# A graph layer whose edges go two ways: 113 picked windows of edges for 100, and 865 gathered chunks for 1125

## The chip, the cores and the metric

The kernel runs on one core of a Trainium2 chip. Its engines each work through their own queue in order: TensorE (PE in the profile; its weight loads are shown apart as PEld), VectorE (DVE), ScalarE (ACT), GpSimd (POOL), and SyncE (SP), which only issues transfers. The metric is the device time of one execution in microseconds (us); several executions of each kernel are timed.

## What is computed

A graph layer over 12,500 nodes of 128 features and 400,000 edges. The edges are sorted by their destination (`dst`), the sources (`src`) are random.

```
Xs  = X[src]
msg = where(edge_type == 0, Xs @ W_data.T + b_data, Xs @ W_control.T + b_control)
agg = segment_sum(msg, dst)
out = relu(agg + X @ W_self.T + b_self)
x   = layernorm(x + out)
```

The kernel sums the source rows first, by destination and by type, and multiplies the sums by the weights afterwards; the number of edges of each type per node, which the biases need, is counted beside it.

## The kernel before

**Data.** The edges are cut into 3125 chunks of 128 (`NC`), in 25 groups of 125 chunks (`NG`, `GC`). A group covers about 500 nodes (`GN`). Each row of x is held as three bf16 parts (384 values, 768 bytes), in SBUF as `x3` and in device memory as `rows3`. The sums of a group stand in a tile `acc` (two types of feature sums, two of counts), 640 nodes wide with a lap into the next group.

**Two ways to sum a chunk.** Each group is cut into windows in turn: a gathered window (kind "p") of 12 or 11 chunks and a picked window (kind "e") of 20 chunks, four of each (`PC`, `EC`, `NE`).

- *Gathered* (`gathered`): for each chunk GpSimd fetches the 128 source rows from `rows3` by an indirect transfer into a tile `msg` (L700); DVE makes for the whole window the 0/1 matrix `psel` that says which edge goes to which of 24 nodes and which type; PE adds the rows with three matmuls of 48 columns (L658) and counts with one (L712) into a bank `sums`. There are 24 `msg` tiles (`AHEAD`), so GpSimd can run ahead.
- *Picked* (`picked`, with `give_slots`): the 2560 edges of a window are sorted by the block of 128 nodes that their source lies in, into 100 cells of 32 places. DVE makes the matrices for that (O, prod, half, rm, rv), PE makes ranks and cells (`rk`), ScalarE copies them, and a broadcast transfer of 800 KB hands the result to all partitions as `pick`. Then PE picks the source rows out of `x3` itself, with 98 matmuls of 384 columns into `got` (L732), four cells at a time; ScalarE copies two results at a time into `emsg` (L743), 12 copies a window; PE adds these by the matrix `esel` with 75 matmuls of 176 columns (L658) and counts with 25 (L761). Edges that find no place in their cell go to 64 spare rows, fetched by one more gather (L747). If a window has more than 64 of these, or a lane more than 7, the flag `bad` is set and a slow path over all 3125 chunks (`long_path`) makes the result.

Both kinds end with a DVE addition of the bank `sums` into `acc` (`accumulate`, L688). The pool of `sums` has two banks, for both kinds together.

**Order.** The program walks over the picked windows w (`pairs`, 100 of them). `merged` weaves into each: its own seven turns of picks, copies and sums, the rank work for the windows w + 2 and w + 3, and the gathered chunks whose place falls there. The chunks are spread evenly over the windows from w = 2 on (`LAG`). Once both kinds of a group are done, the remainder list `rest` holds its lap (`pass_on`) and its finish: load x, turn it, multiply by the three weights and the biases (tile `fin`, L850), normalise, write. The last group is finished in two parts, as its windows close (`soon`).

SP issues the loads of edge data (`load`), the first destination of each window (`first_i`, `near_i`), the transfers `there` and `pick`, the reads of x and the writes of the result.

Of the kernel before, what the change touches and what calls it, by code (L numbers as in the profile page):

```python
# [22 lines left out]
GC = 125  # L23
NG = NC // GC
GN = P * GC * N // E
PC = (12, 11, 11, 11)
PB = 12
EC = 20
CQ = EC // 4
NE = len(PC)  # L30
NWIN = 2 * NE
LAG = 2
DPC = P * N // E
PAD = 10
PW = DPC + 2 * PAD
EW = 88
AW = PW + DPC * (PB - 1)
WMAX = max(AW, EW)
M0 = 50
R = 640  # L40
# [3 lines left out]
NCELL = 4 * NQ  # L44
OVF = 64
TOP = 7
AHEAD = 24
ACC_ROWS = 99 * P
EPS = 1e-5

assert sum(PC) + NE * EC == GC and NC % GC == 0 and NBLK == NCELL - 2 and max(PC) == PB
# [97 lines left out]
def short_path(ctx, tc, const, ident, eps, wT, brow, bad, x, src, dst, etype, ws, bs, out):  # L149
# [12 lines left out]
    def windows(g):  # L162

        c = g * GC
        for i, n in enumerate(PC):
            yield "p", i, c, n
            yield "e", i, c + n, EC
            c += n + EC

    def edges(a, c, n):  # L170
        return a[c * P:(c + n) * P].rearrange("(p c) -> p c", c=n)

    rows_p = NE * PB
    raw = {}
    starts = {k: [c for kind, _, c, _ in windows(0) if kind == k] for k in "pe"}
    assert all(b - a == 31 for k in "pe" for a, b in zip(starts[k][k == "p":], starts[k][1 + (k == "p"):]))

    def load(g, kind):
        names = ("src", "dst", "typ")
        if kind == "e":  # L180
            raw[kind, g] = [ld.tile([P, NE, EC], I32, name=f"e{name}") for name in names]
            c = g * GC + starts["e"][0]
            for t, a in zip(raw[kind, g], (src, dst, etype)):
                at = a[c * P:(c + 31 * (NE - 1)) * P].rearrange("(i k) -> i k", k=31 * P)[:, :EC * P]
                nc.sync.dma_start(out=t[:, :NE - 1, :], in_=at.rearrange("i (p c) -> p i c", c=EC))
                nc.sync.dma_start(out=t[:, NE - 1, :], in_=edges(a, c + 31 * (NE - 1), EC))
        else:
            raw[kind, g] = [ld.tile([rows_p, P], I32, name=f"p{name}") for name in names]
            c = g * GC
            for t, a in zip(raw[kind, g], (src, dst, etype)):  # L190
                nc.sync.dma_start(out=t[:PB, :], in_=a[c * P:(c + PB) * P].rearrange("(c p) -> c p", p=P))
                for i in range(1, NE):
                    b = c + starts["p"][i]
                    nc.sync.dma_start(
                        out=t[i * PB:(i + 1) * PB, :], in_=a[b * P:(b + PB) * P].rearrange("(c p) -> c p", p=P)
                    )


# [15 lines left out]
    near_i = keep.tile([rows_p, NG], I32, name="near_i")  # L214
    for kind, i, c, _ in windows(0):
        if kind == "p":
            nc.sync.dma_start(
                out=near_i[i * PB:(i + 1) * PB, :],
                in_=dst.rearrange("(o g e) -> o g e", o=1, g=NG)[:, :, c * P].to_broadcast([PB, NG]),
            )  # L220
    load(0, "p")

# [109 lines left out]

    worst = keep.tile([P, 3, P], FP, name="worst")
    nc.vector.memset(worst, 0.0)
    over_n = keep.tile([P, NG * NE], BF, name="over_n")

    halves = tmp.tile([1, 2, NG * NWIN], I32, name="halves")
    nc.vector.memset(x3[:, NBLK - 1], 0.0)
# [164 lines left out]
        return [over_before, over_matrix, turn, keep]  # L503

    def give_slots(w):
        g, i = divmod(w, NE)
        blk, blk2, node2, code2, pk = (t[:, i * EC:(i + 1) * EC] for t in codes["e", g])
        s = {}

# [135 lines left out]
        return [(0.6 + a / 1000, lambda a=a: half(a, a + h)) for a in range(0, NCELL, h)]  # L645


    acc, added = {}, []

    def sums():  # L650
        return ps2.tile([P, 512], FP, name="sums")
# [23 lines left out]

    def pass_on(g):

        if g + 1 < NG:
            begin_acc(g + 1)
            added.append(nc.vector.tensor_add(acc[g + 1][:, :, :lap], acc[g + 1][:, :, :lap], acc[g][:, :, GN:]))  # L680

    def accumulate(g, i, ps, wide, width):

        begin_acc(g)
        with tc.issue_after(added[-2].ins) if len(added) > 1 else ExitStack():
            at = nc.vector.value_load(place_i[0:1, g, i:i + 1], min_val=0, max_val=R - WMAX)
        win = acc[g][:, :, bass.ds(at, width)]
        added.append(nc.vector.tensor_add(win, win, ps[:, :4 * wide].rearrange("p (a w) -> p a w", w=wide)[:, :, :width]))  # L688

    def gathered(g, i):  # L690
        n = PC[i]
        s = {}

        def choose():
            sel = sp.tile([P, n, 2 * PW], BF, name="psel")
            s["sel"] = select(sel, near_col, codes["p", g][1][:, i * PB:i * PB + n])

        def chunk(c):
            msg = mp.tile([P, 3 * D], BF, name="msg")
            nc.gpsimd.indirect_dma_start(  # L700
                out=msg, out_offset=None, in_=rows3[:, :],
                in_offset=bass.IndirectOffsetOnAxis(ap=codes["p", g][0][:, i * PB + c:i * PB + c + 1], axis=0),
            )
# [8 lines left out]
            nc.tensor.matmul(cnt, one_col, sel, start=False, stop=(c == n - 1), skip_group_check=True)  # L712
            if c == n - 1:
                accumulate(g, 2 * i, s["ps"], AW, PW + DPC * (n - 1))

        return evenly([lambda c=c: chunk(c) for c in range(n)])

    def picked(w, tiled):

        g, i = divmod(w, NE)  # L720
        s = {"sel": {}, "msg": {}}
        per, pair = 4, 2

# [72 lines left out]

    soon = {NE - 2: (0, 1), NE - 1: (2, 3, 4)}
    assert (starts["p"][NE - 1]) * DPC - PAD >= 2 * (P - 3)  # L800

    def finish(g, ks):
        full = P - 3
# [115 lines left out]


    chunks, closed, rest = {}, {}, []
    for p in range(pairs):
        g, i = divmod(p, NE)
        for c, (_, u) in enumerate(gathered(g, i)):
            at = LAG + (p + (c + 0.5) / PC[i]) * (pairs - LAG) / pairs
            chunks.setdefault(int(at), []).append((at % 1, u))
        closed.setdefault(int(at), []).append(p)

    for w in range(pairs):
        g, i = divmod(w, NE)  # L930
# [193 lines left out]
```

## Time and profile before

| what | value |
|---|---|
| time, median of 3 runs | 2387.49 us (2369.49 to 2400.51) |
| profiled execution: its time / its span | 2371.03 us / 2369.3 us |
| granted TensorE clock, mean | 0.909 |
| gathers (L700), count and mean | 1125, 1147 ns |
| spare-row gathers (L747), count and mean | 100, 1181 ns |
| copies got to emsg (L743), count and mean | 1200, 804 ns |
| additions into acc (L688), count and mean | 200, 470 ns |
| psel (L463), 11 chunks: count and mean | 75, 427 ns |

A line of the profile's groups reads: line of the kernel, engine, operation, tile written and tiles read, count, then busy time and mean of one, then the engine's idle time just before them and what ended it. "issue" stands for idle time in which the profile shows nothing that was waited for. Matmuls overlap, so that the durations of single ones add up to more than PE's time.

### The profile page before, as it was taken

How to read it: one execution, taken by the hardware profiler on the slowest of the kernel's cores; microseconds unless marked ns; L12 is line 12 of the kernel's file. 1: busy time of each engine (PE TensorE's matmuls, PEld its weight loads, DVE VectorE, ACT ScalarE, POOL GpSimd, SP SyncE). 2: the span in 40 equal slices, each digit the busy share in tenths (PEclk: the TensorE clock that was granted, in tenths of full speed). 3: DMA queues.
4: the chain of work that ended last, by engine and by line, in shares of the span. 5: the costliest groups of instructions: out<-in, count | busy, mean ns of one | idle time of the engine just before them, and what ended most of it. 6: DMA issues, size and time to landing. Idle time of an engine off the chain costs nothing.

```text
span 2369.3 us, 70786 instructions
## 1 busy us (share of the span) xinstructions
PE 1863.1 (79%) x28867; PEld 1364.9 (58%) x28867; DVE 1584.0 (67%) x4224; ACT 1229.7 (52%) x2322; POOL 1412.5 (60%) x1243
## 2 busy tenths in 40 slices
PE   0468887887878787888888887888888888887977
PEld 0346665665556565666565565665666665665646
DVE  6747676766666666767676766676667666676753
ACT  3435554555445545545555554555555555545635
POOL 0366665756465565665666665566666665676661
PEclk9879898999889899999999988998989999999979
DMA  7423342333333333333323323333323323233321
GB/s 206 148 80 104 97 107 84 109 91 98 87 96 96 100 100 90 109 97 94 108 85 106 107 86 102 97 98 106 107 83 104 102 88 102 89 101 105 97 87 42
DMA packets 185017, 236.73 MB, mean 100 GB/s; under 512 B 80295, under 2 KB 152282, under 8 KB 184682
## 3 DMA queue, kind: packets, MB, share of 16 engines
q0 software_dynamic: 57200, 115.59, 17.7%
q1 hardware_dynamic: 114418, 109.94, 14.8%
q10 hardware_dynamic: 13064, 6.60, 1.0%
q8 instruction: 228, 3.74, 0.7%
q14 instruction: 107, 0.88, 0.1%
HBM read 215.35 MB, written 16.64 MB: 98 GB/s over the span
## 4 chain that ended last, share of the span: by engine, by line
PE 66%; issue 10%; ACT 10%; DVE 6%; another core or an unknown queue 5%; DMA 1%; SPq 1%; DVEq 0%; ACTq 0%; POOL 0%; POOLq 0%
PE sums L658 32%; PE got L732 22%; ACT emsg L743 9%; PE fin L850 3%; PE rk L601 2%; PE sums L761 2%; PE rk L489 1%; PE sums L712 1%; DVE esel L463 1%; PE rk L537 1%; DVE x L249 1%; PE rk L621 1%; DVE xt L247 0%; PE fin L837 0%
## 5 line engine op out<-in xcount | busy, mean ns | idle before, releaser
L700 POOL DMA_INDIRECT msg<-rows,pidx x1125 | 1290.4, 1147 | 790.3 <-PE sums L658 363.4
L743 ACT CAST emsg<-got 128x768 bf16<-128x768 f32 x1200 | 919.8, 804 | 796.5 <-PE got L732 328.8
L732 PE MATMUL got<-x,pick 128*32 128x384 bf16 x9800 | 659.2, 353 | 238.7 <-ACT emsg L743 145.6
L658 PE MATMUL sums<-esel,emsg 128*128 128x176 bf16 x7200 | 751.3, 255 | 48.6 <-issue 46.0
L658 PEld LDWEIGHTS <-emsg 128*128 128x128 bf16 x7200 | 579.8, 104 | 220.0 <-issue 215.4
L463 DVE TENSOR_TENSOR esel<-code_col,code 128x1408 bf16<-128x1408 bf16 (+1 forms) x300 | 275.0, 917 | 348.9 <-PE sums L658 195.7
L732 PEld LDWEIGHTS <-pick 128*32 128x32 bf16 x9800 | 242.3, 97 | 421.3 <-issue 336.0
L658 PE MATMUL sums<-psel,msg 128*128 128x48 bf16 x3375 | 240.0, 187 | 48.0 <-issue 35.3
L658 PEld LDWEIGHTS <-msg 128*128 128x128 bf16 x3375 | 187.8, 99 | 77.6 <-issue 72.5
L747 POOL DMA_INDIRECT last<-rows,idx x100 | 118.1, 1181 | 139.4 <-DMA pdst<-in_dst_dram 91.4
L712 PE MATMUL sums<-psel,one_col 128*128 128x48 bf16 x1125 | 184.5, 185 | 16.9 <-issue 16.8
L688 DVE TENSOR_TENSOR acc<-acc,sums 128x352 f32 (+1 forms) x200 | 94.0, 470 | 132.5 <-PE sums L658 54.0
L761 PE MATMUL sums<-esel,one_col 128*32 128x176 bf16 x2500 | 168.2, 254 | 16.2 <-issue 14.7
L463 DVE TENSOR_TENSOR O<-cell_col,blk 128x2000 bf16<-128x2000 bf16 x100 | 119.3, 1193 | 55.7 <-PE got L732 27.8
L643 DVE TENSOR_SCALAR pick<-pick,lane_f 128x1600 bf16<-128x1600 bf16 x200 | 125.6, 642 | 14.2 <-DMA pick<-there 13.7
L601 PE MATMUL rk<-rv,O 128*128 128x64 bf16 x2000 | 89.0, 198 | 50.3 <-DVE rv L589 35.0
L761 PEld LDWEIGHTS <-one_col 128*32 128x32 bf16 x2500 | 84.2, 103 | 63.7 <-issue 31.1
L547 DVE TENSOR_REDUCE ahead<-rk 128x100 bf16<-128x500 f32 x100 | 67.5, 675 | 78.7 <-PE got L732 55.7
L712 PEld LDWEIGHTS <-one_col 128*128 128x128 bf16 x1125 | 109.6, 97 | 18.0 <-issue 17.7
L551 DVE TENSOR_TENSOR prod<-O,ahead 128x2000 bf16<-128x2000 bf16 x100 | 119.0, 1190 | 0.0
L601 PEld LDWEIGHTS <-O 128*128 128x128 bf16 x2000 | 73.4, 101 | 67.3 <-issue 54.8
L631 ACT CAST code<-rk 128x50 bf16<-128x50 f32 x100 | 20.3, 203 | 173.8 <-PE got L732 68.0
(170 smaller groups left out, 1998.4 us busy)
## 6 DMA issues: line engine op xcount, KB each, us to landing
pick<-there SPq DMA_DIRECT2D x100, 800.0 KB
msg<-rows,pidx POOLq DMA_INDIRECT x1125
rows<-x SPq DMA_DIRECT2D x6, 1344.0 KB
xs<-in_x_dram SPq DMA_DIRECT2D x99, 62.5 KB
out_dram<-h SPq DMA_DIRECT2D x99, 62.5 KB
xt<-in_x_dram ACTq DMA_DIRECT2D x6, 896.0 KB
psrc<-in_src_dram SPq DMA_DIRECT2D x100, 6.0 KB
pdst<-in_dst_dram SPq DMA_DIRECT2D x100, 6.0 KB
```

Source lines behind the costliest of these rows:

```text
L463: nc.vector.tensor_tensor(sel.rearrange("p n (w t) -> p n w t", t=2), col[:rows].rearrange("p (o w t) -> p o w t", o=1, t=2).to_broadcast( ...
L551: nc.vector.tensor_tensor(prod, s["O"], ahead.rearrange("p (o j) -> p o j", o=1).to_broadcast([P, EC, NCELL]), op=OP.mult)
L601: nc.tensor.matmul(s["rk"][:m, :2 * CAP], s["held"][:, c * NCELL:c * NCELL + m], s["rv"][:, c].rearrange("p v r -> p (v r)"), start=(c == ...
L643: nc.vector.tensor_scalar(t, t, lane_f, None, op0=OP.is_equal)
L658: nc.tensor.matmul(out, msg[:, j * D:(j + 1) * D], sel, start=(start and j == 0), stop=stop, skip_group_check=True)
L688: added.append(nc.vector.tensor_add(win, win, ps[:, :4 * wide].rearrange("p (a w) -> p a w", w=wide)[:, :, :width]))
L700: nc.gpsimd.indirect_dma_start(out=msg, out_offset=None, in_=rows3[:, :], in_offset=bass.IndirectOffsetOnAxis(ap=codes["p", g][0][:, i * P ...
L712: nc.tensor.matmul(cnt, one_col, sel, start=False, stop=(c == n - 1), skip_group_check=True)
L732: nc.tensor.matmul(ps[CAP * a:CAP * (a + 1), :], slots[w]["pick"][:, a * NQ + q, :], x3[:, 4 * q + a - a0].rearrange("p j d -> p (j d)"), ...
L743: nc.scalar.copy(msg, ps[:, :, :3 * D])
L747: nc.gpsimd.indirect_dma_start(out=msg[:OVF, :], out_offset=None, in_=rows3[:, :], in_offset=bass.IndirectOffsetOnAxis(ap=slots[w]["idx"], ...
L761: nc.tensor.matmul(cells_of(s["ps"], EW, 1)[CAP * (q % 4):CAP * (q % 4 + 1), :], one_col[:, :CAP], s["sel"][q], start=(q < 4), stop=(q + 4 ...
```

## The change

Every group has five gathered windows and five picked ones now, of 5 and 20 chunks in turn (`PB`, `EC`, `NE`). In groups with an odd number the last picked window is left out, and its 20 chunks join the gathered window ahead of it, which then has 25 chunks (`PL`). So even groups have 5 picked windows and 25 gathered chunks, odd ones 4 and 45: in all 13 x 5 + 12 x 4 = 113 picked windows and 13 x 25 + 12 x 45 = 865 gathered chunks.

```
-PC = (12, 11, 11, 11)
-PB = 12
+PB = 5
+PL = 25
 EC = 20
-NE = len(PC)
+NE = 5
...
-AHEAD = 24
+AHEAD = 17
...
+    def of_p(g, i):
+        return PL if g % 2 and i == NE - 1 else PB
...
+    each_e = [(g, i) for g in range(NG) for i in range(NE - g % 2)]
...
     def gathered(g, i):
-        n = PC[i]
+        n = of_p(g, i)
...
-            sel = sp.tile([P, n, 2 * PW], BF, name="psel")
+            sel = sp.tile([P, PL, 2 * PW], BF, name="psel")[:, :n]
...
     def picked(w, tiled):
-        g, i = divmod(w, NE)
+        g, i = each_e[w]
...
-    soon = {NE - 2: (0, 1), NE - 1: (2, 3, 4)}
+    soon = {NE - 2: (0, 1, 2), NE - 1: (3, 4)}
...
-    pairs = NG * NE
+    pairs = len(each_e)
...
-    for p in range(pairs):
-        g, i = divmod(p, NE)
-        for c, (_, u) in enumerate(gathered(g, i)):
-            at = LAG + (p + (c + 0.5) / PC[i]) * (pairs - LAG) / pairs
+    total = sum(of_p(g, i) for g in range(NG) for i in range(NE))
+    n = 0
+    for p in range(NG * NE):
+        for _, u in gathered(*divmod(p, NE)):
+            at = LAG + (n + 0.5) * (pairs - LAG) / total
             chunks.setdefault(int(at), []).append((at % 1, u))
+            n += 1
         closed.setdefault(int(at), []).append(p)
```

The loads follow: the edges of gathered windows come in with five transfers per array and group (four before), the last of them always 25 chunks long, and `first_i` and `near_i` have ten and five transfers (eight and four). Chunks are now spread evenly by their number over all windows, so that the gathered work of a group no longer runs beside the picked work of the same group throughout: an even group's 25 chunks take about 3.2 picked windows and an odd group's 45 about 5.8, while the groups have 5 and 4 picked windows. The number of tiles for gathered messages goes from 24 to 17.

More of the change, by code (lines that the diff above doesn't have):

```diff
@@ L36 @@
 EW = 88
-AW = PW + DPC * (PB - 1)
+AW = PW + DPC * (PL - 1)
 WMAX = max(AW, EW)
@@ L46 @@
 TOP = 7
-AHEAD = 24
+AHEAD = 17
 ACC_ROWS = 99 * P
 EPS = 1e-5
-assert sum(PC) + NE * EC == GC and NC % GC == 0 and NBLK == NCELL - 2 and max(PC) == PB
+assert NE * (PB + EC) == GC and PL == PB + EC and NC % GC == 0 and NBLK == NCELL - 2
 @with_exitstack
@@ L164, in windows @@
         c = g * GC
[L165 to L168, printed above, removed]
+        for i in range(NE):
+            yield "p", i, c, PB
+            yield "e", i, c + PB, EC
+            c += PB + EC
+    def of_p(g, i):
+        return PL if g % 2 and i == NE - 1 else PB
     def edges(a, c, n):
         return a[c * P:(c + n) * P].rearrange("(p c) -> p c", c=n)
-    rows_p = NE * PB
+    rows_p = (NE - 1) * PB + PL
+    each_e = [(g, i) for g in range(NG) for i in range(NE - g % 2)]
     raw = {}
     starts = {k: [c for kind, _, c, _ in windows(0) if kind == k] for k in "pe"}
-    assert all(b - a == 31 for k in "pe" for a, b in zip(starts[k][k == "p":], starts[k][1 + (k == "p"):]))
+    gap = PB + EC
     def load(g, kind):
@@ L183, in load @@
             for t, a in zip(raw[kind, g], (src, dst, etype)):
-                at = a[c * P:(c + 31 * (NE - 1)) * P].rearrange("(i k) -> i k", k=31 * P)[:, :EC * P]
+                at = a[c * P:(c + gap * (NE - 1)) * P].rearrange("(i k) -> i k", k=gap * P)[:, :EC * P]
                 nc.sync.dma_start(out=t[:, :NE - 1, :], in_=at.rearrange("i (p c) -> p i c", c=EC))
-                nc.sync.dma_start(out=t[:, NE - 1, :], in_=edges(a, c + 31 * (NE - 1), EC))
+                nc.sync.dma_start(out=t[:, NE - 1, :], in_=edges(a, c + gap * (NE - 1), EC))
         else:
@@ L190, in load @@
             for t, a in zip(raw[kind, g], (src, dst, etype)):
-                nc.sync.dma_start(out=t[:PB, :], in_=a[c * P:(c + PB) * P].rearrange("(c p) -> c p", p=P))
-                for i in range(1, NE):
-                    b = c + starts["p"][i]
+                for i in range(NE):
+                    b, n = c + starts["p"][i], PL if i == NE - 1 else PB
                     nc.sync.dma_start(
-                        out=t[i * PB:(i + 1) * PB, :], in_=a[b * P:(b + PB) * P].rearrange("(c p) -> c p", p=P)
+                        out=t[i * PB:i * PB + n, :], in_=a[b * P:(b + n) * P].rearrange("(c p) -> c p", p=P)
                     )
@@ L216, in short_path @@
         if kind == "p":
+            n = PL if i == NE - 1 else PB
             nc.sync.dma_start(
-                out=near_i[i * PB:(i + 1) * PB, :],
-                in_=dst.rearrange("(o g e) -> o g e", o=1, g=NG)[:, :, c * P].to_broadcast([PB, NG]),
+                out=near_i[i * PB:i * PB + n, :],
+                in_=dst.rearrange("(o g e) -> o g e", o=1, g=NG)[:, :, c * P].to_broadcast([n, NG]),
             )
@@ L334, in short_path @@
     nc.vector.memset(worst, 0.0)
-    over_n = keep.tile([P, NG * NE], BF, name="over_n")
+    over_n = keep.tile([P, len(each_e)], BF, name="over_n")
     halves = tmp.tile([1, 2, NG * NWIN], I32, name="halves")
@@ L645, in pick_matrix @@
         return [(0.6 + a / 1000, lambda a=a: half(a, a + h)) for a in range(0, NCELL, h)]
-    acc, added = {}, []
+    acc, added, parts_in = {}, [], {}
     def sums():
@@ L676, in pass_on @@
     def pass_on(g):
+        assert parts_in[g] == NWIN - g % 2
         if g + 1 < NG:
@@ L684, in accumulate @@
         begin_acc(g)
+        parts_in[g] = parts_in.get(g, 0) + 1
         with tc.issue_after(added[-2].ins) if len(added) > 1 else ExitStack():
@@ L718, in picked @@
     def picked(w, tiled):
-        g, i = divmod(w, NE)
+        g, i = each_e[w]
         s = {"sel": {}, "msg": {}}
@@ L795, in picked @@
         return evenly([lambda t=t: unit(t) for t in range(turns + 1)])
-    soon = {NE - 2: (0, 1), NE - 1: (2, 3, 4)}
-    assert (starts["p"][NE - 1]) * DPC - PAD >= 2 * (P - 3)
+    soon = {NE - 2: (0, 1, 2), NE - 1: (3, 4)}
+    assert (starts["p"][NE - 1]) * DPC - PAD >= 3 * (P - 3)
     def finish(g, ks):
@@ L921, in short_path @@
     chunks, closed, rest = {}, {}, []
-    for p in range(pairs):
-        g, i = divmod(p, NE)
-        for c, (_, u) in enumerate(gathered(g, i)):
-            at = LAG + (p + (c + 0.5) / PC[i]) * (pairs - LAG) / pairs
+    total = sum(of_p(g, i) for g in range(NG) for i in range(NE))
[3 more added lines that the diff above has]
+            at = LAG + (n + 0.5) * (pairs - LAG) / total
             chunks.setdefault(int(at), []).append((at % 1, u))
+            n += 1
         closed.setdefault(int(at), []).append(p)
     for w in range(pairs):
-        g, i = divmod(w, NE)
+        g, i = each_e[w]
         more = []
```

## The prediction

> **What bounds it now.** I read the page first: busy shares, the chain that ended last, the costliest groups.
>
> ```profile
> span 2369.3 us, 70786 instructions
> ...
> PE 1863.1 (79%) x28867; PEld 1364.9 (58%) x28867; DVE 1584.0 (67%) x4224; ACT 1229.7 (52%) x2322; POOL 1412.5 (60%) x1243
> ...
> PE 66%; issue 10%; ACT 10%; DVE 6%; another core or an unknown queue 5%; DMA 1%; SPq 1%; DVEq 0%; ACTq 0%; POOL 0%; POOLq 0%
> PE sums L658 32%; PE got L732 22%; ACT emsg L743 9%; PE fin L850 3%; PE rk L601 2%; PE sums L761 2%; PE rk L489 1%; PE sums L712 1%; DVE esel L463 1%; PE rk L537 1%; DVE x L249 1%; PE rk L621 1%; DVE xt L247 0%; PE fin L837 0%
> ...
> L700 POOL DMA_INDIRECT msg<-rows,pidx x1125 | 1290.4, 1147 | 790.3 <-PE sums L658 363.4
> ```
>
> The chain is TensorE with ScalarE's copies (L743) between; GpSimd has 0% of it, though it is busy 60% of the span. The 790.3 us in which GpSimd idles ahead of its gathers ends mostly at PE's own matmuls: a gather waits for PE to give a message tile back, not PE for a gather. The view of the message tile and of the selection matrix psel says the same from both ends.
>
> ```profile
> L700 POOL DMA_INDIRECT msg<-rows,pidx x1125: 940/950/3073, 100.9 to 2322.4; - x188
> ```
>
> ```profile
> L658 PE MATMUL sums<-psel,msg x3375: 182/183/248, 142.4 to 2353.6; 128*128 128x48 bf16 x199
> ...
> its engine sat idle before it (us, times) until:
>   issue: 73.4, 146
>   DVE acc L688: 7.3, 11
>   DMA msg<-rows,pidx: 2.1, 3
>   DVE esel L463: 2.1, 2
> ```
>
> Gathers run from 100.9 to 2322.4, their matmuls from 142.4 to 2353.6: some 30 to 40 us ahead. In the whole run PE waited 2.1 us for a gather to land. So the change relieves an engine nobody waits for and loads the one in the chain.
>
> Last, busy time by stretches (columns: stretch, length, then PE, weight loads, DVE, ACT, POOL with instruction counts, granted clock, DMA share, GB/s).
>
> ```profile
> 141.80:157.00 15.20, 15.01 (x284) 11.62 (x281) 13.60 (x34) 10.53 (x20) 12.84 (x5) 1.00 0.24 80
> 1000.00:1500.00 500.00, 411.25 (x6397) 300.82 (x6397) 343.85 (x903) 264.15 (x506) 310.37 (x276) 0.91 0.33 99
> 2323.10:2353.50 30.40, 29.76 (x524) 22.86 (x522) 10.41 (x25) 22.36 (x39) 2.46 (x3) 1.00 0.15 44
> ```
>
> The first row is the third picked window, the last row the final two, cut at their last matmuls. They run dense, 15.2 us a window at clock 1.00. The middle row is the steady state: PE busy 82%, clock 0.91, rest gaps.
>
> **The price of a picked window and of a gathered chunk.** From the first chunk matmul to the last, 2353.6 - 142.4 = 2211.2 us hold 98 picked windows: 22.56 us each. In one lie 1125/98 = 11.48 chunks and a quarter of a group's finish.
>
> A chunk on PE: in dense stretches one chunk's four matmuls start 0.10 us after the last chunk's; two chunks from the timeline of PE (start, duration):
>
> ```profile
> 2346.62 0.24 PE L658 MATMUL sums<-psel,msg 128*128 128x48 bf16 x3
> 2346.70 0.18 PE L712 MATMUL sums<-psel,one_col 128*128 128x48 bf16 x1
> 2346.72 0.23 PE L658 MATMUL sums<-psel,msg 128*128 128x48 bf16 x3
> ```
>
> That is at clock 1.00; at 0.91 it is 0.11. The idle rows above add (73.4 + 7.3 + 2.1 + 2.1)/1125 = 0.076. I take 0.19 us. Bounds: 0 (it fills a gap that would be there anyway) and 0.74 (first rival).
>
> The finish of a group: L850 is 3% of the chain, 71 us or 2.8 us a group; PE is busy with the tile "fin" 92.1 us in the 1500 us from 500 to 2000, 16.6 groups, 5.5 us each. I take 4, so 1.0 us a window.
>
> So a picked window without chunks and finish costs 22.56 - 11.48 x 0.19 - 1.0 = 19.4 us, its gaps and its share of halved clock included, for I see nothing that takes them away: a window keeps its twelve ScalarE copies of 804 ns, its DVE work (343.85/500 x 22.56 = 15.5 us) and its chain from put over ScalarE to the next ranks. Bounds: 13.1, a dense window (15.2 less 11 x 0.19), and 21.6, chunks free.
>
> **The change, part by part.**
> - 13 picked windows more (113 for 100): +13 x 19.4 = +252 us.
> - 260 chunks fewer (865 for 1125): -260 x 0.19 = -49 us.
> - GpSimd loses 260 gathers of 1.147 us and gains 13 spare-row gathers of 1.181: -283 us, worth nothing while it is in no chain. DMA loses 260 x 98 KB and gains 13 broadcasts of 800 KB; PE has 2.1 us of gather waits to give back, DVE 13.7 us of waits for the broadcast.
> - DVE: 25 more psel selections and 25 more adds into acc (0.43 + 0.42 us each), 260 chunks less of selection (0.43/11 each): +21 - 10 us, plus 13 windows, on an engine that then stands near 69%: hidden in PE's time.
> - AHEAD 24 to 17: 7.8 chunks a window make 17 tiles a lead of two windows, some 45 us, against a gather of 1 us: hidden. With the cover gone each gather would cost up to 1.147 us.
> - Loads: a group has 15 small transfers of gathered edges for 12, each some 0.6 us of SP's queue (the chain at the start has first_i issues of 0.66 to 0.92), ahead of "there" and "pick" in that queue only in one window of a group. SP waits for work most of the time: 0 in the loop. At the start first_i and near_i have 3 transfers more, ahead of the first window: +2 us, between 0 and 7 (one such landing took 6.79).
> - Tail: the last gathered window but one now closes with the last picked window, so two finishing batches (3 and 2 tiles) stand behind it instead of one of 3. The old tail is 15.7 us (2353.6 to 2369.3); a tile costs PE 0.8 us there, DVE 0.65, ScalarE 0.4: +6, between 0 and 16.
> - Order on the engines: in a middle window PE has the same sequence (picks of 16, counts, 12 sums) with 7 or 8 chunks let in for 11 or 12, so I expect no new wait from the order.
>
> Sum: 252 - 49 + 2 + 6 = +211 us on the profiled 2371.0 (its span 2369.3 and 1.7 around it): 2582. That execution lies 16 us below the median of the runs shown, 2387.49; taking half of that in, I forecast 2590.
>
> **Two rules weighed.** DVE's largest operation, the product over 2,000 elements (L551), lasted 1179 to 1200 ns in all of its 100 executions, with GpSimd at work or not. The Trainium skill, GPSIMD Engine Reference, section Key points, says that GpSimd shares its SBUF interfaces with VectorE and contends with it; by that, fewer gathers would speed DVE up. The row shows no slowing to win back, so the sum with the rule and without is the same here.
>
> PE is 79% busy and PEld 58%. The Trainium skill, Perfetto Trace Analysis, section Identifying the Most-Contended Engine, says that matmul busy share tells little and that weight-load share is the better sign of headroom; by it TensorE has 40% free, the 13 windows would sink into that, and the time would stay near 2371. The chain (66% PE) and the gaps' enders speak against it: PE's gaps are hand-overs inside a window, which come with each new window.
>
> **Rivals.**
> 1. Gather traffic itself slows PE: the gap between a steady window and a dense one is the chunks' doing. Then a chunk costs (22.56 - 1.0 - 13.1)/11.48 = 0.74 us and a window 13.1: 13 x 13.1 - 260 x 0.74 + 8 = -14, so 2357: not slower. The place is the wait ahead of L732 and L658 while a gather is in flight; it decides from 0.685 us a chunk (20 of them then cost a window's worth), and only from 0.82 is it over 2% faster. For it: the final two windows have GpSimd idle (2.46 of 30.4 us) and run dense. Against: the window from 141.8 runs as dense with GpSimd busy 12.84 of 15.2 us.
> 2. The new windows cost no more than dense ones, since other engines have caught up: 13 x 13.1 - 49 + 8 = +122, 2493.
> 3. PSUM: the pool "sums" has two banks. The 25-chunk run of an odd group holds one for 25/7.8 = 3.2 windows, so picked windows there share the other, and the first count must wait for DVE's add (0.52 us, in DVE's queue). For it: PE already waited 11 times for that add, 7.3 us. Against: 16 picks stand between. At 1 us a window, 12 groups x 3 = +36: 2626 on the forecast.
> 4. The change overflows its own limits: 64 spare rows a window, 7 a lane; beyond them the slow path over 3125 chunks runs. Three gathers of 1.147 us in each make an estimate of over 10 ms. Counted in the reference's inputs, the fullest of the 113 windows has 63 spare rows (57 before) and no lane over 5. So it stays on the fast path.
>
> **How the numbers follow.** Forecast, 2590 with the ends, 0.70; rival 3 added to it, 0.10; rival 2, 0.10; rival 1, 0.08, a little of it beyond 2% (0.03); rival 4 and the unforeseen, 0.02. Chunks free and both ends at their worst give 2371 + 280 + 23 = 2674. The range runs from 2500 to 2650: half of rival 2 is inside (2493 on the profiled base, 2509 on the median's); left out are rivals 1 and 4, the other half of rival 2 (0.05) and the far end of free chunks (0.05). A measurement tells about 2% from no change (the runs before spread over 1.3%). Slower by over 2% starts at 2435: 0.90; within 2%, 0.06; faster, 0.04.
>
> **What would show it.** After: TensorE's share in the chain stays two thirds, GpSimd busy near 1130 us and under half of the span, DVE near 1784 (1584 + 13 x 14.5 + 11), ScalarE near 1380 (1230 + 13 x 11.9, 264.15/500 of a window each); first to last chunk matmul over 111 windows at 21.7 us each (19.4 + 7.8 x 0.19 + 0.9). A period near 19.7 us would mean rival 1 ((2211 - 22)/111); near 20.9, rival 2 ((2211 + 114)/111); many waits of PE's counts (L761 before) for acc, rival 3. I am wrong if the gaps ahead of L732 and L658 shrink with the number of chunks.

## The result, and the profile after

| | before | after |
|---|---|---|
| median (runs) | 2378.49 us (4) | 2216.28 us (4) |
| lowest to highest | 2367.23 to 2400.51 | 2202.22 to 2217.37 |
| ratio, 95% interval | | 0.9306 (0.925 to 0.9363) |
| profiled span, granted clock | 2369.3, 0.909 | 2215.4, 0.957 |

The change makes the kernel 7% faster; 2590 us was forecast. These lines of the page of after answer to those shown of before: busy times, the chain that ended last, the gathers. In the kernel after, the picks stand at L740 (L732 before), the additions at L664 (L658), the gathers at L708 (L700).

```profile
PE 1877.4 (85%) x30869; PEld 1393.5 (63%) x30869; DVE 1737.6 (78%) x4706; ACT 1353.9 (61%) x2556; POOL 1193.9 (54%) x996
...
PE 69%; DVE 10%; ACT 8%; issue 6%; another core or an unknown queue 3%; DMA 1%; DVEq 0%; POOL 0%; ACTq 0%; SPq 0%; POOLq 0%
...
L708 POOL DMA_INDIRECT msg<-rows,pidx x865 | 1056.2, 1221 | 843.8 <-PE sums L664 512.9
```

PE has 2002 matmuls more, yet its busy time rose by only 14 us (1863.1 to 1877.4), and its idle time in the span fell from 506 to 338. GpSimd waits longer for PE than before, and still has 0% of the chain. By those readings the change should have cost time. The steady stretch (columns as in the prediction) shows the same:

```profile
1000.00:1500.00 500.00, 443.00 (x7345) 329.30 (x7344) 402.75 (x1091) 314.32 (x599) 283.32 (x237) 0.96 0.33 100
```

In 500 us PE does 7345 matmuls in place of 6397, at clock 0.96 in place of 0.91. The period of a picked window, from last chunk matmul to last chunk matmul, fell from 22.6 to 18.6 us. The view of waits (engine, tile and line, what was waited for; us in all, times, longest) has only few rows that account for it. First before, then after:

```profile
PE got L732 <- ACT emsg L743: 145.6, 192, 8.4
PE sums L658 <- issue: 87.1, 186, 4.6
PE got L732 <- issue: 80.9, 134, 2.8
```

```profile
PE got L740 <- ACT emsg L751: 127.9, 171, 4.1
PE got L740 <- issue: 48.7, 71, 3.6
PE sums L664 <- issue: 36.0, 74, 2.9
```

What shrinks most is idle time under "issue", for which the trace shows nothing that was waited for. Most of these stalls lie between matmuls of one kind, in the middle of a run, as in this stretch of PE's timeline before (start, duration, and in brackets the idle time ahead):

```profile
1000.37 0.70 PE L658 MATMUL sums<-esel,emsg 128*128 128x176 bf16 x7
1002.10 0.24 PE L658 MATMUL sums<-esel,emsg 128*128 128x176 bf16 x1 [1.02 <-issue]
1002.80 0.24 PE L658 MATMUL sums<-esel,emsg 128*128 128x176 bf16 x1 [0.47 <-issue]
```

Counted over the trace of each kernel (idle stretches of PE over 60 ns under "issue", from 120 us after the start to 60 us before the end; called *stalls* below), they are 502 with 220 us before, 347 of them between matmuls of one kind, and 190 with 92 us after. The time that PE spent at half clock fell with them, from 432 to 194 us.

The sum, on the profiled runs: 13 windows less 260 chunks are some +150 us of matmuls at full clock (13.7 a window, from the first experiment: 15.97 us of PE busy a window, less 11.25 chunks of 0.11 and 1.0 of finish; less 260 x 0.11). Of this, busy time shows +14, so that about 136 us came back in busy time. PE was busy for 336 us at half clock before and for 150 after, so that the clock can have given back half of the difference, 93 us. The other 43 or so are not taken apart by any run; PE's busy time is broken off less often (922 unbroken stretches before, 496 after), and a matmul that stands alone counts with its full length. Idle time gave 168 more, some 128 of it under "issue" and 40 in waits for ScalarE: 150 - 136 - 168 = -154, which is the difference of the spans.

### The profile page after: what moved, and what is told of

It is laid out like the page before. It is cut to its first block, busy times and chain, and to the rows that moved or that the text cites. A ratio compares the mean times of both kernels' runs of the same rounds, so it can differ in the third digit from the quotient of the medians.

```text
span 2215.4 us, 75505 instructions
## 1 busy us (share of the span) xinstructions
PE 1877.4 (85%) x30869; PEld 1393.5 (63%) x30869; DVE 1737.6 (78%) x4706; ACT 1353.9 (61%) x2556; POOL 1193.9 (54%) x996
## 4 chain that ended last, share of the span: by engine, by line
PE 69%; DVE 10%; ACT 8%; issue 6%; another core or an unknown queue 3%; DMA 1%; DVEq 0%; POOL 0%; ACTq 0%; SPq 0%; POOLq 0%
PE sums L664 32%; PE got L740 24%; ACT emsg L751 7%; PE sums L769 3%; PE rk L607 3%; DVE esel L469 2%; PE fin L858 2%; PE rk L495 2%; PE rk L543 1%; DVE pick L649 1%; PE sums L720 1%; DVE rv L595 1%; DVE found L566 1%; PE rk L627 1%
## 5 line engine op out<-in xcount | busy, mean ns | idle before, releaser
L708 POOL DMA_INDIRECT msg<-rows,pidx x865 | 1056.2, 1221 | 843.8 <-PE sums L664 512.9
L751 ACT CAST emsg<-got 128x768 bf16<-128x768 f32 x1356 | 1029.8, 802 | 545.6 <-PE got L740 314.4
L740 PE MATMUL got<-x,pick 128*32 128x384 bf16 x11074 | 691.8, 342 | 183.5 <-ACT emsg L751 127.9
L664 PE MATMUL sums<-esel,emsg 128*128 128x176 bf16 x8136 | 788.8, 246 | 20.7 <-issue 19.6
L664 PEld LDWEIGHTS <-emsg 128*128 128x128 bf16 x8136 | 615.0, 100 | 200.1 <-issue 198.0
L740 PEld LDWEIGHTS <-pick 128*32 128x32 bf16 x11074 | 259.2, 96 | 351.0 <-issue 242.0
L469 DVE TENSOR_TENSOR esel<-code_col,code 128x1408 bf16<-128x1408 bf16 x339 | 310.5, 916 | 196.3 <-PE sums L664 142.7
L664 PE MATMUL sums<-psel,msg 128*128 128x48 bf16 x2595 | 200.8, 185 | 16.9 <-issue 13.4
L769 PE MATMUL sums<-esel,one_col 128*32 128x176 bf16 x2825 | 186.6, 247 | 1.7 <-DVE idx L506 0.6
L664 PEld LDWEIGHTS <-msg 128*128 128x128 bf16 x2595 | 153.5, 98 | 33.5 <-issue 28.5
L696 DVE TENSOR_TENSOR acc<-acc,sums 128x352 f32 (+2 forms) x238 | 101.6, 427 | 89.5 <-PE sums L664 40.8
L720 PE MATMUL sums<-psel,one_col 128*128 128x48 bf16 x865 | 152.4, 184 | 6.9 <-issue 6.8
L769 PEld LDWEIGHTS <-one_col 128*32 128x32 bf16 x2825 | 93.7, 100 | 47.1 <-issue 7.2
```

The costliest lines, as they stand in the source:

```text
L469: nc.vector.tensor_tensor(sel.rearrange("p n (w t) -> p n w t", t=2), col[:rows].rearrange("p (o w t) -> p o w t", o=1, t=2).to_broadcast( ...
L664: nc.tensor.matmul(out, msg[:, j * D:(j + 1) * D], sel, start=(start and j == 0), stop=stop, skip_group_check=True)
L708: nc.gpsimd.indirect_dma_start(out=msg, out_offset=None, in_=rows3[:, :], in_offset=bass.IndirectOffsetOnAxis(ap=codes["p", g][0][:, i * P ...
L740: nc.tensor.matmul(ps[CAP * a:CAP * (a + 1), :], slots[w]["pick"][:, a * NQ + q, :], x3[:, 4 * q + a - a0].rearrange("p j d -> p (j d)"), ...
L751: nc.scalar.copy(msg, ps[:, :, :3 * D])
L769: nc.tensor.matmul(cells_of(s["ps"], EW, 1)[CAP * (q % 4):CAP * (q % 4 + 1), :], one_col[:, :CAP], s["sel"][q], start=(q < 4), stop=(q + 4 ...
```

## The experiments

**Theory and rivals.** The theory: a gather holds PE back though no wait names it, so that the number of gathers decides. Rivals: the new layout or the new order did it; the 17 tiles did it; the bytes of the gathers did it; GpSimd's being busy did it; waits for gathered tiles did it, under another name.

The runs lay on chips of two kinds. On three chips the kernel before took 2418 to 2426 us (the first result, 2378, is like these): here *dear* chips, since gathers turned out dear there. On two others the same kernel took 1977 and 1982 us: *cheap* chips. Each chip was used on one occasion only, so that the runs do not tell the chip from the occasion. Ratios compare runs on the same chip only.

### On a dear chip: which part of the change

**No gathers for chunks.** All reads of gathered tiles go to one fixed tile; matmuls, selections and additions stay as they are. Nothing else of before is changed.

```
-            msg = mp.tile([P, 3 * D], BF, name="msg")
-            nc.gpsimd.indirect_dma_start(...)
+            msg = still[0]
```

> The kernel before without its 1125 gathers: the chunk matmuls read one fixed message tile instead (sums of gathered edges are left wrong), all PE, DVE and ScalarE work stays. Theory T (gather traffic slows TensorE: its stalls without a wait and the halved clock behind them are the gathers' doing): the stalls of some 130 us and most of the halved clock go, 2100 to 2230 us. Theory L (the new layout of the gathered windows made the kernel faster, traffic does not matter): 2340 to 2390 us, stalls as before. My forecast's view (PE waited 2.1 us for gathers, all else a window's own): 2360 to 2390.

Measured: 1754.75 us, ratio 0.7242 (0.7212 to 0.7272). The page:

```profile
span 1752.8 us, 68519 instructions
...
PE 1605.4 (92%) x28867; PEld 1245.3 (71%) x28867; DVE 1551.9 (89%) x4225; ACT 1212.3 (69%) x2322; POOL 111.6 (6%) x118
...
PE 46%; DVE 36%; DMA 7%; ACT 4%; issue 3%; DVEq 2%; SPq 1%; ACTq 0%
```

The same 28867 matmuls take 258 us less PE time, at a granted clock of 0.993, and 8 stalls are left (1.1 us). So 1125 gathers cost 667 us, 0.59 us each, where the prediction had 0.08 for each (a chunk's 0.19 less 0.11 of matmuls). Against the profile of before shown above, the span is 616 us shorter: 258 in PE's busy time, 225 in idle time under "issue", 152 in PE's waits for ScalarE, with some 20 lost again in other waits. The chain is now shared by PE and DVE.

**The new layout with the old amounts.** After's code with four picked windows in every group: 100 picked windows, 1125 chunks, 17 tiles, chunks spread by their number. (The last windows of the last group are added after its first tiles were finished; the amount of work is the same.)

```
-        return PL if g % 2 and i == NE - 1 else PB
+        return PL if i == NE - 1 else PB
-    each_e = [(g, i) for g in range(NG) for i in range(NE - g % 2)]
+    each_e = [(g, i) for g in range(NG) for i in range(NE - 1)]
```

> The changed kernel with four picked windows in every group, not only the odd ones: 100 picked windows and 1125 chunks as before the change, in the layout of after (gathered windows of 5, 5, 5, 5 and 25 chunks, 17 tiles). Theory T: the number of gathers decides, so near the time before, 2340 to 2400 us. Theory L: the layout decides, and 13 windows fewer save some 13 x 15 us less 260 chunks at 0.2: 2050 to 2150 us.

Measured: 2419.44 us, ratio 0.9993 (0.994 to 1.0046); 456 stalls with 217 us. Layout and order are worth nothing.

**Five picked windows in every group.** The same two lines the other way: 125 picked windows, 625 chunks.

```
+        return PB
+    each_e = [(g, i) for g in range(NG) for i in range(NE)]
```

> The changed kernel with five picked windows in every group: 125 picked windows, 625 chunks, layout of after without the long gathered window. Theory T: another 240 gathers fewer, time falls on: 2050 to 2150 us. Theory L: 12 windows more at some 17 us less 240 chunks at 0.2: 2340 to 2400 us. A bound by PE alone (dense window 13.1 us, chunk 0.19) would be 2216 + 157 - 46 = 2327.

Measured: 2192.2 us, ratio 0.9047 (0.9006 to 0.9088); 74 stalls with 33 us. This version beats both kernels: after was at 0.9306 (0.925 to 0.9363) and, on another dear chip, 0.9247 (0.9127 to 0.9368). It is not compared with after on one chip.

**17 tiles alone.** Before with `AHEAD = 17`.

> The kernel before with 17 message tiles for 24, nothing else. Theory T: GpSimd runs less far ahead, same number of gathers: within 1% of before, 2355 to 2400. Theory L with the tiles as its cause: a part of the gain, 2200 to 2330.

Measured: 2406.09 us, ratio 0.9919 (0.9882 to 0.9956); 449 stalls with 236 us. Under one per cent of the seven.

What follows: the number of gathers decides. The price is not a constant, though. Taking 14.3 us a picked window from the run without gathers (13.7 and its idle time of 0.6) and 0.11 a chunk's matmuls, the kernels without their gathers would take 1755 (before), 1912 (after) and 2057 us (all five); what lies above is 667 for 1125 gathers, 341 for 865 (0.9306 x 2421.63 = 2253.6) and 135 for 625: 0.59, 0.39 and 0.22 us a gather. These are estimates. The first gathers that are taken away are worth the most.

### On a cheap chip: what of a gather

The next four kernels were meant to part transfers, bytes and GpSimd. They fell on a cheap chip (before 1977.3 us there), with one execution of each.

**Gathers made, but not read**: PE reads the fixed tile, the gathers go to tiles apart. **The same, 64 bytes a row** in place of 768.

```
+            msg = still[0]
+            apart = mp.tile([P, 3 * D], BF, name="msg")
             nc.gpsimd.indirect_dma_start(
-                out=msg, out_offset=None, in_=rows3[:, :],
+                out=apart, out_offset=None, in_=rows3[:, :],
```

> As e1 (kernel before, chunk matmuls read one fixed tile), but the 1125 gathers run again, each into one of 24 tiles that nothing reads: the sums of gathered edges are left wrong. TensorE no longer waits for a gather and GpSimd no longer for TensorE. Theory W (the coupling by waits and tile returns costs the time): as e1, 1740 to 1800 us. Theories D (the bytes moved) and G (GpSimd's making of descriptors): as the kernel before, 2300 to 2430.

> As e5, but each gather fetches rows of 64 bytes for 768, a twelfth of the bytes with the same 1125 instructions of 128 indices; nothing reads them. Theory D: nearly all of the cost goes, 1760 to 1850 us. Theory G: the cost stays, 2250 to 2430. Theory W: 1740 to 1800, as e5.

Measured: 2498.26 and 2486.82 us, slower than before, with one stall of 0.2 us in the first and none in the second. The waits of the first:

```profile
PE sums L658 <- DMA last<-rows,idx: 684.3, 41, 27.2
```

and GpSimd's timeline around one of them (start, duration):

```profile
1003.77 0.95 POOL L707 DMA_INDIRECT msg<-rows,pidx  x1 [0.30 <-issue]
1005.02 1.77 POOL L707 DMA_INDIRECT msg<-rows,pidx  x1 [0.30 <-issue]
1007.10 2.44 POOL L754 DMA_INDIRECT last<-rows,idx  x1 [0.30 <-issue]
1009.85 1.61 POOL L707 DMA_INDIRECT msg<-rows,pidx  x1 [0.30 <-issue]
```

Nothing reads the tiles, so nothing paces the gathers: all that a group's indices allow are released at once, and the spare rows (`last`), needed in every window, stand behind up to some 30 of them in GpSimd's queue. A side effect of the edit, but a real one: it names a wait that the tile pool kept small.

**The same bytes by plain transfers** from SP, unread. **GpSimd busy without transfers**: a copy of 128 x 384 in place of each gather.

```
+            nc.sync.dma_start(out=apart, in_=rows3[at:at + P, :])
```

```
+            nc.gpsimd.tensor_copy(apart, col.to_broadcast([P, 3 * D]))
```

> As e5, but the 98 KB of each chunk come by a plain transfer issued by SP, 128 rows of 768 bytes that lie one after another, and GpSimd has no part in it; nothing reads them. Theory D: the cost stays in large part, 2150 to 2430 us. Theory G: the cost goes, 1750 to 1900 (SP has 1125 more issues of some 0.6 us in its queue, ahead of pick, which could add up to 100). Theory W: as e5.

> As e1, but GpSimd makes 1125 copies of 128 x 384 from the index column into the 24 tiles where it gathered; no transfer, nothing reads them. Theory G in the form that GpSimd's presence on SBUF slows the others: 1900 to 2400 us, DVE's operations longer. Theory D, or G in the form of descriptors only: 1740 to 1800 as e1.

Measured: 1790.05 and 1997.16 us. The bytes are nearly free, as far as 1790 lies near the 1755 of the run without gathers, which was on a dear chip. The copies are not; the page of that run has

```profile
PE 1671.7 (84%) x28867; PEld 1285.7 (64%) x28867; DVE 1802.1 (90%) x4225; ACT 1214.2 (61%) x2322; POOL 906.5 (45%) x1243
```

DVE, with the same work, is busy 1802 us against 1553 with the plain transfers. The runs of this kernel with gathers have 1558 to 1584, so that it is GpSimd's computing, and hardly its gathering, that slows DVE here.

**The two kernels and the spare rows**, on another cheap chip (before 1982.39 us): before again, after again, gathers unread with the spare rows taken from fixed tiles, and before with its gathers and only the spare rows fixed.

```
-            msg = s["msg"][NQ - 1] = two.tile([P, 3 * D], BF, name="last")
-            nc.gpsimd.indirect_dma_start(...)
+            s["msg"][NQ - 1] = lasts[w % 2]
```

> The kernel before once more, unchanged, for its profile beside the next three on one chip: the three chips so far gave 2378, 2422 and 1977 us for it. Where it is near 2400, TensorE should show stalls without a wait of some 200 us, at a halved clock a fifth of the time; where it is near 1980, hardly any.

> The changed kernel once more, unchanged, on the same chip as g1. If g1 is near 2400: ratio 0.93 again, 2230 to 2260 us. If g1 is near 1980, the stalls that the change removes are not there, and 13 windows at 14 us less 260 chunks at 0.2 to 0.5 us count: 2010 to 2110 us, slower.

> As e5 (1125 gathers of full rows into tiles that nothing reads, chunk matmuls on a fixed tile), and the 100 gathers of spare rows are left out too (the last matmuls of a window read two fixed tiles), since in e5 TensorE waited 684 us for a spare-row gather that stood in GpSimd's queue behind a burst of others. Theory D/G (the running of gathers slows TensorE whatever waits for them): 1950 to 2430, as g1. Theory W (it is waits on gathers that cost): 1740 to 1800.

> The kernel before with its 1125 gathers read as they are, and only the 100 spare-row gathers left out (two fixed tiles in their place; sums of those rows wrong). If the spare rows behind other gathers in GpSimd's queue cost the time: 1750 to 1900. If the gathers of chunks themselves do: within 3% of g1.

Measured: 1986.52 (0.3% above the other runs of the same kernel); 1951.8, ratio 0.9839 (0.979 to 0.9887); 1866.48, ratio 0.9409 (0.9369 to 0.9448); 1872.19, ratio 0.9438 (0.9351 to 0.9524). Before has 3 stalls (0.3 us) here, and in its waits stands a row that on dear chips is not among the large ones:

```profile
PE sums L658 <- DMA last<-rows,idx: 165.6, 47, 15.1
```

Where PE is not stalled, it presumably asks for the spare rows sooner, and they stand behind chunk gathers in GpSimd's queue. Without them the kernel is 110 us faster. So on a cheap chip the change gains 1.6%, and the 1125 gathers cost 190 to 230 us (1982 less the 1790 with plain transfers or the 1755 without gathers, the latter from a dear chip), about half of it by that queue.

### On a dear chip: what of a gather, once more

Theories T, R and Q as in the texts below (descriptors, bytes, waits). The edits are those shown: after; gathers unread with no spare rows to wait for; the same with 64 bytes a row; plain transfers.

> The kernel after, the yardstick of this set. On a chip where the kernel before takes about 2400 us: a ratio near 0.93, with PE stalls that wait for nothing summing to 60 to 120 us; where it takes about 1980 us: near 0.98, without such stalls.

> The kernel before with all 1125 gathers made but not read, and with the spare rows taken from a fixed tile, so that no matmul waits for any gather: the amount of matmuls is the same. On a chip where the kernel before takes about 2400 us: T and R (gathers slow PE without a wait) expect 2150 to 2400 us, with PE stalls that wait for nothing of 100 us or more; Q (it is the waits) expects 1750 to 1900 and hardly a stall. On a chip of about 1980 us: 1870 as seen there, no stalls.

> As the run with whole rows unread, but each gather moves 64 bytes a row in place of 768. On a chip of about 2400 us: T (descriptors) expects the same time within 2% as with whole rows; R (bytes) expects 1750 to 1900 us; Q the same as T, but both at 1750 to 1900. On a chip of about 1980 us: about 1870 by all three, since GpSimd's own queue of 1125 gathers at 1.25 us ends last there.

> The kernel before with each gather replaced by a plain transfer of as many bytes from SP, unread; the spare rows are gathered as before. On a chip of about 2400 us: R (bytes) expects 2150 to 2400 us; T and Q expect 1760 to 1850, with a clock above 0.97 and few stalls. On a chip of about 1980 us: 1790 as seen there.

Measured, with before at 2426.04 us:

| run | us | ratio (95%) | clock | stalls |
|---|---|---|---|---|
| after | 2246.36 | 0.9247 (0.9127 to 0.9368) | 0.953 | 176, 99 us |
| unread, 768 bytes | 3198.39 | 1.3167 (1.3001 to 1.3333) | 0.762 | 750, 1006 us |
| unread, 64 bytes | 3208.31 | 1.3207 (1.3042 to 1.3373) | 0.760 | 735, 1090 us |
| plain transfers | 1789.1 | 0.7365 (0.7278 to 0.7452) | 0.984 | 27, 3 us |

No theory had foreseen 3200 us, but they are told apart: no matmul waits for a gather, so it is not the waits; a twelfth of the bytes changes nothing, and all the bytes by another way end 34 us above the run without gathers. It is GpSimd's indirect transfers as such. (Whether plain transfers issued by GpSimd would do the same is not tested.) The kernel of the second row took 1866 us on the cheap chip. Its busy time in two stretches on the dear chip, one with no gathers (POOL x0), one with 36 of them back to back:

```profile
1380.00:1438.00 58.00, 56.92 (x1025) 44.47 (x1017) 51.41 (x145) 38.88 (x69) 0.00 (x0) 0.97 0.14 48
1438.00:1485.00 47.00, 13.84 (x124) 6.66 (x122) 8.73 (x21) 6.00 (x17) 35.58 (x36) 0.57 0.36 104
```

and the second stretch of the same kernel on the cheap chip:

```profile
1438.00:1485.00 47.00, 44.63 (x782) 34.45 (x775) 40.27 (x110) 31.99 (x66) 38.01 (x30) 0.96 0.44 128
```

Matmuls (first bracket) fall from 1025 in 58 us to 124 in 47; on the cheap chip there are 782. Over all long runs of gathers (9 and more, from 5 us after their start), PE starts 1.2 matmuls a us on the dear chip, 14.5 outside them, and 16.2 inside them on the cheap chip. DVE's and ScalarE's instructions fall as far (145 to 21, 69 to 17), though these also wait for PE. The timeline inside the second stretch:

```profile
1449.09 0.52 PE L741 MATMUL got<-x,pick 128*32 128x384 bf16 x3 [1.16 <-issue]
...
1449.38 0.94 POOL L707 DMA_INDIRECT msg<-rows,pidx  x1 [0.30 <-issue]
1449.82 0.10 PEld L741 LDWEIGHTS <-pick 128*32 128x32 bf16 x1 [0.60 <-issue]
1450.52 0.52 PE L741 MATMUL got<-x,pick 128*32 128x384 bf16 x2 [0.91 <-issue]
1450.54 0.10 PEld L741 LDWEIGHTS <-pick 128*32 128x32 bf16 x1 [0.62 <-issue]
1450.63 0.95 POOL L707 DMA_INDIRECT msg<-rows,pidx  x1 [0.31 <-issue]
1451.24 0.10 PEld L741 LDWEIGHTS <-pick 128*32 128x32 bf16 x1 [0.61 <-issue]
```

PE's weight loads come one by one, about 0.7 us apart, and its matmuls up to three together, 0.7 or 1.4 us apart, inside a run of picks that elsewhere start four together every 0.15 us. Nothing is waited for.

So in before the stalls must lie where gathers are close together, and they do. Share of time lost to stalls, by the number of gathers, spare rows' too, begun in the 6 us ahead of the stall's start (in brackets the us that the kernel spends in that state):

| gathers in 6 us | before | after | all five |
|---|---|---|---|
| 0 or 1 | 0% (73) | 0% (173) | 0.1% (460) |
| 2 | 1% (263) | 1% (486) | 0.4% (769) |
| 3 | 4% (879) | 3% (893) | 2% (650) |
| 4 | 17% (881) | 12% (467) | 12% (127) |
| 5 | 32% (93) | 18% (16) | - (5) |

On the cheap chip closeness does nothing: before spends 1010 us there with four gathers in 6 us and 391 with five, and has 0.3 us of stalls.

The table fits the falling price per gather: fewer gathers are also further apart. In the kernels that read their gathers a long run seems to stop itself, because PE, stalled, returns no tiles; unread, nothing stops it, and at four or five in 6 us about 70% of the time goes to stalls.

### Spacing alone

Two or four small writes on GpSimd (one partition, 200 elements) ahead of every chunk's gather.

```
+            for _ in range(2):
+                nc.gpsimd.memset(pauses[0], 0.0)
```

> The kernel before with two small writes on GpSimd (one partition, 200 elements, estimated 0.2 to 0.4 us each) ahead of every chunk's gather, so that gathers that were released together follow each other at 1.7 us or more in place of 1.25. Number, layout and reads of the gathers are as before. On a chip where the kernel before takes about 2400 us: S (spacing decides) expects the PE stalls that wait for nothing to fall from about 220 us to under 110, the time with four or more gathers begun in the last 6 us to shrink from about 970 us to under 300, and the time to fall to 2150 to 2330 us; N (their number decides, about 0.6 us each) expects the stalls to stay at 180 to 250 us and the time at 2380 to 2480. On a chip of about 1980 us: no stalls to save, 1980 to 2080 by both, GpSimd's writes being added work.

> The kernel after with four such small writes ahead of every chunk's gather: 865 chunks' gathers follow each other at 2 us or more. On a chip where the kernel before takes about 2400 us: S expects stalls of 25 to 60 us in place of about 95 and a ratio to before of 0.87 to 0.92 (the kernel after was at 0.925 to 0.931); N expects stalls of 80 to 110 us and a ratio of 0.92 to 0.96. On a chip of about 1980 us: a ratio of 0.98 to 1.03 by both.

Measured, with before at 2417.94 us: 2771.93 us, ratio 1.1448 (1.1399 to 1.1496), and 2816.98, ratio 1.1642 (1.1598 to 1.1686). Both theories missed the times. Stalls fell from 220 to 123 us and from 92 (99 in the second run of after) to 37, at the same number of gathers. GpSimd's timeline of the first tells why it is slower:

```profile
1499.53 0.95 POOL L706 DMA_INDIRECT msg<-rows,pidx  x1 [0.30 <-issue]
1500.47 4.02 POOL L705 MEMSET pause<- 1x200 bf16 x13
1504.92 1.30 POOL L706 DMA_INDIRECT msg<-rows,pidx  x1 [0.43 <-issue]
```

The writes, which wait for nothing, stand together ahead of their gathers, 13 of them in the row above and more elsewhere, instead of one pair before each. GpSimd was busy 1945.8 us, and the spare rows came late: PE waited 541 us for `last` (165.6 in before on a cheap chip). Stalls inside that wait are not seen, so the lower count is weak evidence for spacing. The experiment is inconclusive on it. It does answer another rival, that GpSimd's being busy stalls PE: the second kernel spends 765 us with at most one gather begun in the last 6 us, and in these GpSimd is busy for 62% of the time, mostly with the small writes, PE for 73%, and there is no stall. Larger GpSimd work was not run on a dear chip. For the design, a queue that holds a transfer which PE needs in every window is no place for filler.

## Why the prediction was wrong

**What bounds the kernel.** That PE and its hand-overs to ScalarE are the chain was right, and stays so (69%). That nobody waits for GpSimd was right as to waits: 2.1 us. The step from there to "an engine nobody waits for", GpSimd's -283 us "worth nothing", is the step that failed. A cost that takes no wait has no row that names the one who causes it. The chain had a share for it all the same, "issue 10%". The prediction took up only the 73.4 us ahead of the chunks' own matmuls and passed over the rest; the share is 6% after and 3% without gathers.

**The price of a chunk, 0.19 us.** This term was mis-sized: gathers cost 0.59 us each on average beside their 0.11 of matmuls, the 260 removed ones more. Rival 1 was the right mechanism with the right test, 0.74 us a chunk and 13.1 a window. It was given 0.08, and even its 2357 was too high by 140: it spread the cost evenly over the chunks, where the traces show that stalls grow with the gathers' closeness and that half clock comes with them. With its window and its ends, the profiled difference of -154 asks for (13 x 13.1 + 8 + 154)/260 = 1.28 us a removed chunk.

**Why rival 1 was put aside.** For it stood the final windows, dense with GpSimd idle. Against it stood the window from 141.8 to 157, dense with GpSimd busy 12.84 of 15.2 us. The weighing read the busy time and not the count beside it, "x5". GpSimd's timeline there:

```profile
142.94 1.71 POOL L700 DMA_INDIRECT msg<-rows,pidx  x1 [11.16 <-PE sums L658]
144.96 6.14 POOL L747 DMA_INDIRECT last<-rows,idx  x1 [0.30 <-issue]
151.40 3.07 POOL L700 DMA_INDIRECT msg<-rows,pidx  x1 [0.30 <-PE got L732]
154.78 0.95 POOL L700 DMA_INDIRECT msg<-rows,pidx  x1 [0.30 <-issue]
156.03 2.62 POOL L700 DMA_INDIRECT msg<-rows,pidx  x1 [0.30 <-issue]
```

Five gathers in 15.2 us, the spare rows' among them, are two in 6 us, where the table above has 1% of stalls. The steady row has 276 in 500 us, 3.3 in 6 us. The counterexample was a window with few gathers that lasted long. The window right behind it stood in the same view, and the prediction did not show it (columns as there):

```profile
157.00:187.10 30.10, 22.22 (x284) 13.92 (x283) 16.00 (x45) 11.21 (x22) 21.16 (x20) 0.77 0.33 92
```

It has the same 284 matmuls, 20 gathers in place of 5, and takes 30.1 us in place of 15.2.

**The price of a window, 19.4 us.** It held the gathers' cost in its gaps and its clock ("I see nothing that takes them away"). Without gathers a window is 14.3. Rival 2's dense price, 13.1, was near that, and wrong as a forecast because it left the chunks at 0.19. Its sum is also off: 13 x 13.1 - 49 + 8 is +129, not +122, so that it stood for 2500 on the profiled base, the lower end of the range.

**Other steps.** The ends: +6 for the tail, measured 15.7 to 23 us, +7; the start +2, measured -2 (first window closed at 102.6, then at 100.8). The fewer tiles hidden: shown (17 tiles alone, 0.9919). No new wait from the order: shown (all four, 0.9993). Rival 3, banks: PE's counts (L769) idled 1.7 us in all, so no. Rival 4 did not come. DVE 1737.6 for 1784 and ScalarE 1353.9 for 1380 were a little over; GpSimd 1193.9 for 1130, since a gather took 1221 ns for 1147. The period of 18.6 us lies below all that was named (21.7, 20.9, 19.7). The last sentence of the prediction named the sign by which it would be wrong, gaps ahead of the picks and sums that shrink with the chunks: L732's "issue" went from 80.9 to 48.7, L658's from 87.1 to 36.0.

**The rules weighed.** The Trainium skill, Perfetto Trace Analysis, section Identifying the Most-Contended Engine, would have given 2371 by PE's headroom of weight loads: nearer than the forecast, though not by what happened, since the windows did not sink into idle time that stayed; the idle time itself went. GPSIMD Engine Reference, section Key points, is borne out where GpSimd computes (DVE 1802 us against 1553) and hardly where it gathers (1565 us on the cheap chip with gathers unread, 1553 with plain transfers).

## What to carry to other kernels

Price an engine's work by taking it out of a run, not by who waits for it: a row of idle time under "issue", spread over identical instructions, is a cost without a name, and the count of instructions in a stretch says more than their busy time. Look at how closely GpSimd's gathers follow each other, and keep what each window needs, however small, from standing behind them in its queue. Say which kind of chip a gain was measured on: this one is 7% or 1.6%.

## What the runs showed of the hardware

- **Two kinds of chips.** The same kernel took 1977 and 1982 us on two chips and 2418 to 2426 on three. Most gathers last as long on both (median 950 and 957 ns in the kernel before, 0.30 us between them), and with plain transfers in their place the kernel takes 1789 and 1790 us. What differs is whether PE's instructions come slowly while gathers follow closely. Why, stays open. The transfers that the profile lists under the kind "instruction" do not get slower: within the long runs of unread gathers on the dear chip 21 of them took 0.69 us on average, the 294 outside 0.88.
- **The halved clock.** In the record of the granted clock of before, in steps of 3.41 us, all 50 steps at full clock with PE busy under half were followed by half clock, 19 of 31 at 50 to 60% busy, 7 of 127 at 60 to 80%, none of 336 above. The Trainium skill, TensorE: Matmul & The Clock Gate, section HAM oscillation, describes this for idle gaps longer than about 3.4 us; here shorter gaps are enough when they add up to half a step: in 49 of the 50 steps the longest gap that PE had was 0.5 to 2.8 us. So stalls, with a median of 0.36 us, cost twice: 432 us of before were run at half clock, 26 us without gathers.
- **A gather's time does not depend on its bytes.** 64 or 768 bytes a row: the same 0.98 us on GpSimd on average and nearly the same end, 3208 and 3198 us.
